# Attention block with f32 products: each product of 128 columns of weights issued as two of 64

## The chip, the cores and the metric

The kernel runs on one core of one Trainium2 chip, in float32 throughout. The metric is the time of one execution in device microseconds. A core has TensorE for matrix products (PE in the profile; its weight loads are listed apart as PEld), VectorE (DVE), ScalarE (ACT), GpSimd (POOL) and the queue of SyncE (SP), which here only issues transfers.

## The reference

An attention block on images: a group norm over 8 groups of channels, the projections to q, k and v, attention with 4 heads over the 1024 pixels of each image, a projection back, and the residual. The input is 16 images of 512 channels by 32 x 32 pixels, so a head has 128 channels.

```python
b, c, h, w = x.shape                      # 16, 512, 32, 32
xg = x.reshape(b, NUM_GROUPS, -1)         # 8 groups
...
xn = ((xg - mu) * jax.lax.rsqrt(var + EPS)).reshape(b, c, h, w)
xn = xn * norm_gamma[:, None, None] + norm_beta[:, None, None]
qkv = jnp.einsum('oc,bchw->bohw', qkv_w, xn) + qkv_b[:, None, None]
q, k, v = jnp.split(qkv, 3, axis=1)
...
scale = dh ** (-0.5)
attn = jax.nn.softmax(jnp.einsum('bhnd,bhmd->bhnm', q, k) * scale, axis=-1)
out = jnp.einsum('bhnm,bhmd->bhnd', attn, v)
out = out.transpose(0, 1, 3, 2).reshape(b, c, h, w)
out = jnp.einsum('oc,bchw->bohw', proj_w, out) + proj_b[:, None, None]
return x + out
```

## The kernel before, in words

The work is a fast path, followed by a general branch that is taken only if a softmax sum left its safe range; the profiled execution does not take it. All that follows is the fast path.

**Attention (L843 to L950).** The main loop runs over 512 steps: 16 images, 4 heads, 8 blocks of 128 keys. A step has two halves of 512 queries. In each half `scores` (L846) multiplies a block of 128 keys, as the weights, with 512 queries, as the moving operand, into a bank of PSUM called `s`; ScalarE takes the exponential of it into `p` (L852); and `weighted_sum` (L942) multiplies a block of `v`, as the weights, with the `p` of the step before, and accumulates over the 8 key blocks in `po`. There are two `s` banks, and one `po` of two banks, which ScalarE copies out to `o` (L949) at the end of a head. VectorE adds up the `p` of a head in `tot` (L858, L860); their sums give the softmax denominators, which are inverted, spread over the partitions by way of DRAM, and multiplied into `o` by VectorE. From the second image on, the blocks of `v` lie with a step of four elements between columns (`v_block`, L793).

**Projections (L472 to L700).** The products with the projection weights for q and k (two sites per image), v and the output are done by a scheme with seven products in place of eight, on two levels. `two_levels` runs four groups of outer products (`OUTER`); in each group `strassen` runs seven units `p1` to `p7` in the order `ORDER`, and `mm` (L606) issues one product per outer product of the group: 128 x 128 weights, 256 moving columns. Units write the PSUM banks called `qk_x`, `qk_y`, `v_x`, `v_y`, `pp_x` and `pp_y`. Between two units ScalarE copies an `x` bank out (`kept_copy`, L486: tiles `qk_p`, `qk_u` and the like) and later units go on accumulating in the same bank. VectorE combines the parts (L630, L679). The v product of the first image is on one level (`v_units`, L732), and so is the output projection of the last one (`last_projection`, L1031, tiles `lx`, `ly`, `lz`).

**Order.** The projections of the next image, and the output projection of the image before, are spread over the main loop by `plan_head`: a list of units for each step of a head, half of which run after each half step. TensorE's instructions are in program order: scores, weighted sum, one or two units, and so on. Copies and exponentials are marked with a raised priority, so that they come early in the order of their engine.

**Small products.** The group norm averages over channels with products of a 128 x 128 matrix `avg` with 2 or 4 columns (L83, L88). `warm` (L1149) issues products of `avg` with itself at the start. `bias_of_v` (L965) and `last_division` (L904, L922) use one or 512 columns of the moving operand. The check for the general branch, on the tile `most` (L1077, L1078), has weights of a single column.

Each call of `nc.tensor.matmul` in f32 gives two weight loads and two passes in the records.

Of the kernel before, what the change touches and what calls it, by code (L numbers as in the profile page):

```python
# [16 lines left out]
P = 128  # L17
# [8 lines left out]


URGENT = 40


class Norm:
# [29 lines left out]
    def group_steps(self, mv, first=0):  # L61


        nc, gn, k = self.nc, self.gn, mv.shape[1]
        t = {}

        def tile_(n):
            t[n] = gn.tile([P, k], F32, tag=n, name=n)
            return t[n]

        def bank(n):
            t[n] = self.ps.tile([P, HALF], F32, tag=self.tag, name=n)[:, :k]
            return t[n]

        def scale():
            ins = nc.vector.tensor_mul(tile_("sc"), t["rstd"], self.gamma[:, first : first + k])
            self.result = t["mu"], t["sc"]
            return ins


        return [
            lambda: nc.vector.tensor_copy(tile_("mean"), mv[:, :, 0]),
            lambda: nc.tensor.matmul(bank("pm"), self.avg, t["mean"], start=True, stop=True),  # L83
            lambda: nc.vector.tensor_sub(tile_("d"), t["mean"], t["pm"]),
            lambda: nc.vector.tensor_mul(tile_("d2"), t["d"], t["d"]),
            lambda: nc.vector.tensor_add(tile_("vv"), t["d2"], mv[:, :, 1]),
            lambda: nc.vector.tensor_copy(tile_("mu"), t["pm"]),
            lambda: nc.tensor.matmul(bank("pv"), self.avg, t["vv"], start=True, stop=True),  # L88
            lambda: nc.vector.tensor_scalar_add(tile_("ve"), t["pv"], EPS),
            lambda: nc.gpsimd.tensor_tensor(  # L90
                tile_("rstd"), t["ve"], self.neghalf[:, :k], ALU.pow
            ),
            scale,
        ]
# [92 lines left out]
def fast_path(ctx, tc, x, sources, out, consts, flag, dims):  # L187
# [335 lines left out]
    def two_levels(name, site, b, blocks, finish, sums="make", homes="BBBB", prepare=None):  # L523
# [58 lines left out]
        def group_units(g):  # L582
            group = OUTER[g]
            n = len(group)
            have = haves[g]

            def weights():
                have["w"] = group_weights(site, g, b == 0 and site in range(PAIRS))

            def load(m):  # L590
                h = homes.find(homes[g], g + 1)
                if sums == "load" and h > 0:
                    nc.sync.dma_start(sum_tile(h, m), inner_kept[b, h, m])

            def inner_sum(m):
                if sums != "load" and m not in have:
                    make_sum(g, m)

            def inner(i, m):
                return inner_block(g, i, m)  # L600

            def mm(acc, j, first):
                an, bn = FACTORS[j]
                t, slot = SLOTS[an]
                for i in range(n):
                    nc.tensor.matmul(  # L606
                        acc[:, ts(i, Q)], have["w"][t][:, i, slot, :], inner(i, bn),
                        start=(first and i == 0), stop=True, skip_group_check=True,
                    )

            def out_(which, a, c=None):
                row, half = int(which[1]) - 1, int(which[2]) - 1
                if g not in R and opening and g == len(OUTER) - 1:

                    t = opool.tile([P, N], F32, tag="o", name=f"{name}_r{g}")
                    R[g] = t.rearrange("p (i r m) -> p i r m", i=1, r=2)
                elif g not in R:
                    R[g] = rpool.tile(
                        [P, 2, 2, HALF], F32, tag=f"r{g % 3}", name=f"{name}_r{g}"
                    )  # L620
                dst = R[g][:, :n, row, ts(half, Q)]

                def view(t):
                    return t[:, : n * Q].rearrange("p (i q) -> p i q", q=Q)

                with tc.high_priority(URGENT):
                    if c is None:
                        nc.scalar.copy(dst, view(a))
                    else:
                        nc.vector.tensor_add(dst, view(a), view(c))  # L630

            p1, p2, p6, p5, p7, p4, p3 = strassen(f"{name}_{g}", mm, out_, n * Q)

            def unit(*steps):
                def one():
                    for f in steps:
                        f()
                    with placed():
                        for _ in range(min(len(pending), 2 if g == len(OUTER) - 1 else 1)):
                            pending.pop(0)()  # L640
                return one

            def end():
                combine(g)
                if g == len(OUTER) - 1:
                    with placed():
                        run(pending)
                    pending.clear()


            return [
                unit(
                    weights, lambda: first_sums((1,)) if g == 0 and sums == "load" else None,
                    lambda: inner_sum("t1"), lambda: inner_sum("t2"), p1,
                ),
                unit(lambda: inner_sum("t3"), p2), unit(lambda: inner_sum("t4"), p6),
                unit(lambda: load("t2"), lambda: ready(g), p5), unit(lambda: load("t1"), p7),
                unit(lambda: load("t3"), p4), unit(lambda: load("t4"), p3, end),
            ]
# [64 lines left out]
    def v_units(b, jj):  # L724
# [3 lines left out]
        def mm(acc, i, first):  # L728
            wi, bn = wv[FACTORS[i][0]], FACTORS[i][1]
            for g in range(2):  # L730
                for k in range(KC):
                    nc.tensor.matmul(  # L732
                        acc[:, ts(g, HC)], xb[b][bn][k][:, ts(2 * jj + g, P)], wi[:, k, :],
                        start=(first and g == 0 and k == 0), stop=(k == KC - 1),
                        skip_group_check=True,
                    )
# [106 lines left out]
    def scores(s, half):  # L843
        b, h, j = where(s)
        sc = ps_s.tile([P, HALF], F32, tag="s", name=f"s_{s}_{half}")
        nc.tensor.matmul(  # L846
            sc, ks[b, h][:, ts(j, P)], qs[b, h][:, ts(half, HALF)], start=True, stop=True
        )
        if half == 0:
            ps[s] = ppool.tile([P, N], F32, tag="p", name=f"p_{s}")  # L850
# [47 lines left out]
    def last_division(b, h):  # L898
# [2 lines left out]
        t = tot.pop((b, h))  # L901
        acc = ps_s.tile([P, HALF], F32, tag="s", name="l_last")
        for j in range(NB):
            nc.tensor.matmul(  # L904
                acc[:, j : j + 1], t[:, ts(j, P)], ones_sq[:, 0:1], start=(j == 0), stop=True,
                skip_group_check=True,
            )
        r = lpool.tile([P, NB], F32, tag="part", name="r_last")
# [10 lines left out]
            )  # L919
        for half in range(NH2):  # L920
            rows = ps_s.tile([P, HALF], F32, tag="s", name=f"rows_{half}")
            nc.tensor.matmul(  # L922
                rows, ones_sq, blocks[:, ts(half, n), :].rearrange("p j q -> p (j q)"),
                start=True, stop=True,
            )
            i = ts(half, HALF)
            nc.vector.tensor_mul(os_[b, h][:, i], os_[b, h][:, i], rows)
# [9 lines left out]
    def weighted_sum(s, half):  # L937
        b, h, j = where(s)
        if j == 0 and half == 0:
            po[b, h] = ps_o.tile([P, N], F32, tag="o", name=f"po_{b}_{h}")  # L940
        i = ts(half, HALF)
        nc.tensor.matmul(  # L942
            po[b, h][:, i], v_block(b, h, j), ps[s][:, i],
            start=(j == 0), stop=(j == NB - 1),
        )
        if j == NB - 1:
            if (b, h) not in os_:
                os_[b, h] = opool.tile([P, N], F32, tag="o", name=f"o_{b}_{h}")
            last_eviction[b] = nc.scalar.copy(os_[b, h][:, i], po[b, h][:, i])  # L949
# [9 lines left out]
    def bias_of_v(o):  # L959
# [2 lines left out]
        half, r = divmod(o, 2)  # L962
        for c in range(NCC):
            block = stage["proj"][f"a{half + 1}{c // KC + 1}"]
            nc.tensor.matmul(  # L965
                acc[:, 0:1], block[:, ts(r * KC + c % KC, P)], vb_sb[:, c : c + 1],
                start=(c == 0), stop=(c == NCC - 1),
            )
        nc.vector.tensor_add(
# [53 lines left out]
    def last_projection(b):  # L1023
# [4 lines left out]

        def mm(acc, r, p, first):
            for k in range(KC):  # L1030
                nc.tensor.matmul(  # L1031
                    acc, late["w"][p][:, ds((r * KC + k) * P, P)], bl[FACTORS[p][1]][k],
                    start=(first and k == 0), stop=(k == KC - 1), skip_group_check=True,
                )

# [38 lines left out]
            add(1, r, 1, kept_["u3", r], False)  # L1074
            add(1, r, 1, y_[r], True)
        most = ps_s.tile([P, HALF], F32, tag="s", name="most")
        nc.tensor.matmul(most[:1, :1], total, ones, start=True, stop=False)  # L1077
        nc.tensor.matmul(most[:1, :1], span, ones_sq[:, 0:1], start=False, stop=True)  # L1078
        ok = gn.tile([1, 1], F32, tag="fine", name="fine")
        nc.vector.tensor_scalar(ok, most[:1, :1], LIMIT, None, ALU.is_le)  # L1080
        fine.append(ok)
# [67 lines left out]
    def warm(n, name):  # L1149

        acc = ps_s.tile([P, HALF], F32, tag="s", name=name)
        for _ in range(n):
            ins = nc.tensor.matmul(acc[:, :P], avg, avg, start=True, stop=True)  # L1153
            tc.keep_in_program_order(ins)

    def open_image():
# [247 lines left out]
```

## Time and profile before

| what | value |
|---|---|
| median of two runs (3171.86 and 3172.45 us) | 3172.15 us |
| span of the profiled execution, first to last instruction | 3170.7 us |
| mean granted TensorE clock in it | 1.000 |
| PE busy, records | 3159.9 us, 10524 |
| PEld busy, records | 2190.7 us, 10524 |
| DVE / ACT / POOL busy | 2633.6 / 1439.7 / 517.7 us |
| mean share of the 16 DMA engines that the two largest queues use | 28.8% and 19.2% |

The profiled execution has a span of its own, 3170.7 us; its whole time is not listed beside it, and the two runs lie 1.2 and 1.8 us above that span. A line of the profile's groups reads: line of the kernel, engine, operation, what is written and read, rows and columns of weights (128\*128), shape of the output, number of records, then the busy time of the group, the mean time of one record, and the idle time of the engine ahead of them with what ended it. Busy times are of the union: records that overlap are counted once, so a mean can be longer than the distance from one start to the next.

### The profile page before, as it was taken

To read this page: it belongs to the slowest core of one execution; us is meant where nothing else is said; L and a number is where in the kernel's file an instruction comes from. 1 tells how busy PE (TensorE), PEld (TensorE's weight loads), DVE (VectorE), ACT (ScalarE), POOL (GpSimd) and SP (SyncE) were. 2 spreads that over 40 slices of the span, in tenths; PEclk is the share of its full clock that TensorE was granted. 3 is DMA by queue.
4 is the path that set the end of the run, shared out by engine and by line. 5 is a ranking of instruction groups with operands and counts; after the bars stand their busy time and mean duration, and the time that the engine had idled before them with its cause. 6 is when DMAs were issued, how large, how long until landed. Compare 5 with 4: busy or idle time off the path is not lost.

```text
span 3170.7 us, 34267 instructions
## 1 busy us (share of the span) xinstructions
PE 3159.9 (100%) x10524; PEld 2190.7 (69%) x10524; DVE 2633.6 (83%) x4639; ACT 1439.7 (45%) x2712; POOL 517.7 (16%) x898
## 2 busy tenths in 40 slices
PE   9999999999999999999999999999999999999999
PEld 7566676677766676777767767677676776766764
DVE  9878879788897888878788787987879978788784
ACT  3535435354353543545435453453534545344342
POOL 0011221111211112211122111222012221122200
PEclk9999999999999999999999999999999999999999
DMA  5554554555545455454554545555455564555531
GB/s 177 185 190 154 188 172 154 171 153 192 171 164 162 153 185 175 167 167 145 191 172 162 171 145 187 171 172 172 144 175 169 176 189 134 174 162 186 179 116 41
DMA packets 210333, 524.32 MB, mean 165 GB/s; under 512 B 32096, under 2 KB 65376, under 8 KB 210144
## 3 DMA queue, kind: packets, MB, share of 16 engines
q1 hardware_dynamic: 132896, 282.12, 28.8%
q0 software_dynamic: 64000, 204.54, 19.2%
q10 hardware_dynamic: 13248, 35.39, 3.5%
q8 instruction: 87, 1.43, 0.2%
q14 instruction: 102, 0.84, 0.1%
HBM read 388.77 MB, written 133.17 MB: 165 GB/s over the span
## 4 chain that ended last, share of the span: by engine, by line
PE 96%; DVE 3%; DMA 0%; issue 0%; POOL 0%; SPq 0%; ACT 0%; DVEq 0%; POOLq 0%
PE po L942 27%; PE s L846 27%; PE qk_x L606 12%; PE qk_y L606 9%; PE pp_x L606 6%; PE v_x L606 6%; PE pp_y L606 4%; PE v_y L606 4%; PE lx L1031 0%; DVE qk_t L574 0%; PE ly L1031 0%; PE warm L1153 0%; DVE tot L860 0%; DVE qk L714 0%; DVE qk_r L630 0%
## 5 line engine op out<-in xcount | busy, mean ns | idle before, releaser
L942 PE MATMUL po<-p,v 128*128 128x512 f32 x2048 | 1049.5, 594 | 0.7 <-ACT p L852 0.7
L846 PE MATMUL s<-qk,qk 128*128 128x512 f32 x2048 | 1047.4, 593 | 0.3 <-DVE qk L714 0.3
L852 ACT ACTIVATE p<-s 128x512 f32<-128x512 f32 x1024 | 610.9, 597 | 961.0 <-PE s L846 957.2
L942 PEld LDWEIGHTS po<-p,v 128*128 128x128 f32 x2048 | 603.6, 302 | 322.7 <-issue 214.5
L860 DVE TENSOR_TENSOR tot<-tot,p 128x1024 f32<-128x1024 f32 x385 | 469.0, 1218 | 158.4 <-ACT p L852 156.3
L846 PEld LDWEIGHTS s<-qk,qk 128*128 128x128 f32 x2048 | 387.7, 190 | 88.6 <-issue 29.9
L606 PEld LDWEIGHTS qk_x<-qk_t,w 128*128 128x128 f32 x1344 | 251.8, 190 | 166.1 <-issue 75.3
L606 PE MATMUL qk_x<-qk_t,w 128*128 128x256 f32 x1344 | 356.3, 382 | 0.1
L486 ACT COPY qk_u<-qk_x 128x512 f32<-128x512 f32 (+1 forms) x256 | 136.3, 533 | 229.2 <-PE qk_x L606 229.2
L779 POOL DMA_DIRECT2D vd<-vu x120 | 66.7, 557 | 899.8 <-DVE vu L771 897.9
L630 DVE TENSOR_TENSOR qk_r<-qk_y,qk_u 128x512 f32<-128x512 f32 (+1 forms) x256 | 157.7, 616 | 34.7 <-ACT qk_u L486 21.6
L580 POOL DMA_DIRECT2D kept_t<-qk_t x240 | 129.4, 540 | 278.4 <-DVE qk_t L574 211.9
L606 PEld LDWEIGHTS pp_x<-pp_t,w_proj 128*128 128x128 f32 x630 | 117.2, 190 | 74.7 <-issue 32.3
L784 POOL DMA_DIRECT2D v<-vd x240 | 140.6, 593 | 167.1 <-DMA vd<-vu 70.3
L630 DVE TENSOR_TENSOR v_r<-v_y,v_u 128x512 f32<-128x512 f32 (+1 forms) x120 | 76.0, 633 | 110.6 <-ACT v_u L486 80.3
L606 PE MATMUL pp_x<-pp_t,w_proj 128*128 128x256 f32 x630 | 167.8, 383 | 0.0
L606 PE MATMUL v_x<-v_t,w_v 128*128 128x256 f32 x630 | 166.6, 381 | 0.0
L830 POOL DMA_DIRECT2D out_y<-y x120 | 66.0, 550 | 604.2 <-DVE y L829 602.4
L606 PEld LDWEIGHTS v_x<-v_t,w_v 128*128 128x128 f32 x630 | 118.4, 190 | 55.3 <-issue 19.1
L606 PE MATMUL qk_y<-x,w 128*128 128x256 f32 x512 | 142.1, 379 | 0.0
L714 DVE SCALAR_TENSOR_TENSOR qk<-qk_r,qkb_sb,qk_r 128x512 f32<-128x512 f32 x192 | 137.5, 743 | 1.6
L486 ACT COPY v_u<-v_x 128x512 f32<-128x512 f32 (+1 forms) x124 | 66.3, 535 | 157.1 <-PE v_x L606 130.3
(217 smaller groups left out, 4487.2 us busy)
## 6 DMA issues: line engine op xcount, KB each, us to landing
w<-kept SPq DMA_DIRECT2D x90, 512.0 KB, 3.7
kept_t<-qk_t POOLq DMA_DIRECT2D x180, 256.0 KB, 3.3
v_t<-kept_t SPq DMA_DIRECT2D x180, 256.0 KB, 2.9
w<-kept SPq DMA_DIRECT2D x90, 384.0 KB, 3.4
rinv<-row ACTq DMA_DIRECT2D x63, 512.0 KB, 4.9
x<-in_x POOLq DMA_DIRECT2D x60, 512.0 KB, 4.6
vd<-vu POOLq DMA_DIRECT2D x120, 256.0 KB, 3.1
v<-vd POOLq DMA_DIRECT2D x240, 128.0 KB, 4.2
```

What stands on the lines that cost most here:

```text
L486: nc.scalar.copy(t[n][:, :width], t["x"][:, :width])
L580: nc.gpsimd.dma_start(t, to)
L606: nc.tensor.matmul(acc[:, ts(i, Q)], have["w"][t][:, i, slot, :], inner(i, bn), start=(first and i == 0), stop=True, skip_group_check=True,)
L630: nc.vector.tensor_add(dst, view(a), view(c))
L714: nc.vector.scalar_tensor_tensor(st[b, h][:, ts(half, HALF)], a, qkb_sb[:, i : i + 1], c, ALU.add, ALU.add)
L779: nc.gpsimd.dma_start(rows[which][ts(h, P), :], u)
L784: nc.gpsimd.dma_start(vs[b, pair][ts(q, BLK), half].rearrange("m h (k i) j -> m (h k) (i j)", k=n), rows[which].rearrange("(k m) (q e) -> ...
L830: nc.gpsimd.dma_start(out[b, ts(o, P), ts(half, HALF)], t)
L846: nc.tensor.matmul(sc, ks[b, h][:, ts(j, P)], qs[b, h][:, ts(half, HALF)], start=True, stop=True)
L852: exps[s] = nc.scalar.activation(ps[s][:, ts(half, HALF)], sc, AF.Exp, scale=SCALE)
L860: added[b, h, j] = nc.vector.tensor_add(tot[b, h][:, i], tot[b, h][:, i], ps[s][:, i])
L942: nc.tensor.matmul(po[b, h][:, i], v_block(b, h, j), ps[s][:, i], start=(j == 0), stop=(j == NB - 1),)
```

## The change

A helper takes the place of `nc.tensor.matmul` in the fast path. Where the weights have 128 columns it issues two products: columns 0 to 63 of the weights into partitions 0 to 63 of the output, then columns 64 to 127 into partitions 64 to 127, with the same moving operand and the same flags. Weights with fewer than 128 columns (the two products on `most`) are issued as before. The instruction that it returns is the second of the two. The general branch keeps its calls.

```diff
+def halves_of(nc, out, lhsT, rhs, **flags):
+
+    m = lhsT.shape[-1]
+    if m < P:
+        return nc.tensor.matmul(out, lhsT, rhs, **flags)
+    for d in range(2):
+        cols = ts(d, P // 2)
+        ins = nc.tensor.matmul(out[cols], lhsT[:, cols], rhs, **flags)
+    return ins
...
-            lambda: nc.tensor.matmul(bank("pm"), self.avg, t["mean"], start=True, stop=True),
+            lambda: halves_of(nc, bank("pm"), self.avg, t["mean"], start=True, stop=True),
...
                 for i in range(n):
-                    nc.tensor.matmul(
-                        acc[:, ts(i, Q)], have["w"][t][:, i, slot, :], inner(i, bn),
+                    halves_of(
+            nc, acc[:, ts(i, Q)], have["w"][t][:, i, slot, :], inner(i, bn),
                         start=(first and i == 0), stop=True, skip_group_check=True,
                     )
...
-        nc.tensor.matmul(
-            sc, ks[b, h][:, ts(j, P)], qs[b, h][:, ts(half, HALF)], start=True, stop=True
+        halves_of(
+            nc, sc, ks[b, h][:, ts(j, P)], qs[b, h][:, ts(half, HALF)], start=True, stop=True
         )
...
-        nc.tensor.matmul(
-            po[b, h][:, i], v_block(b, h, j), ps[s][:, i],
+        halves_of(
+            nc, po[b, h][:, i], v_block(b, h, j), ps[s][:, i],
             start=(j == 0), stop=(j == NB - 1),
         )
...
-            ins = nc.tensor.matmul(acc[:, :P], avg, avg, start=True, stop=True)
+            ins = halves_of(nc, acc[:, :P], avg, avg, start=True, stop=True)
```

The same replacement is made in the second averaging product (L88), in `v_units`, `last_division`, `bias_of_v` and `last_projection`.

More of the change, by code (lines that the diff above doesn't have):

```diff
@@ L87, in group_steps @@
             lambda: nc.vector.tensor_copy(tile_("mu"), t["pm"]),
-            lambda: nc.tensor.matmul(bank("pv"), self.avg, t["vv"], start=True, stop=True),
+            lambda: halves_of(nc, bank("pv"), self.avg, t["vv"], start=True, stop=True),
             lambda: nc.vector.tensor_scalar_add(tile_("ve"), t["pv"], EPS),
@@ L731, in mm @@
                 for k in range(KC):
-                    nc.tensor.matmul(
-                        acc[:, ts(g, HC)], xb[b][bn][k][:, ts(2 * jj + g, P)], wi[:, k, :],
+                    halves_of(
+            nc, acc[:, ts(g, HC)], xb[b][bn][k][:, ts(2 * jj + g, P)], wi[:, k, :],
                         start=(first and g == 0 and k == 0), stop=(k == KC - 1),
@@ L903, in last_division @@
         for j in range(NB):
-            nc.tensor.matmul(
-                acc[:, j : j + 1], t[:, ts(j, P)], ones_sq[:, 0:1], start=(j == 0), stop=True,
+            halves_of(
+            nc, acc[:, j : j + 1], t[:, ts(j, P)], ones_sq[:, 0:1], start=(j == 0), stop=True,
                 skip_group_check=True,
@@ L921, in last_division @@
             rows = ps_s.tile([P, HALF], F32, tag="s", name=f"rows_{half}")
-            nc.tensor.matmul(
-                rows, ones_sq, blocks[:, ts(half, n), :].rearrange("p j q -> p (j q)"),
+            halves_of(
+            nc, rows, ones_sq, blocks[:, ts(half, n), :].rearrange("p j q -> p (j q)"),
                 start=True, stop=True,
@@ L941, in weighted_sum @@
         i = ts(half, HALF)
-        nc.tensor.matmul(
-            po[b, h][:, i], v_block(b, h, j), ps[s][:, i],
+        halves_of(
+            nc, po[b, h][:, i], v_block(b, h, j), ps[s][:, i],
             start=(j == 0), stop=(j == NB - 1),
@@ L964, in bias_of_v @@
             block = stage["proj"][f"a{half + 1}{c // KC + 1}"]
-            nc.tensor.matmul(
-                acc[:, 0:1], block[:, ts(r * KC + c % KC, P)], vb_sb[:, c : c + 1],
+            halves_of(
+            nc, acc[:, 0:1], block[:, ts(r * KC + c % KC, P)], vb_sb[:, c : c + 1],
                 start=(c == 0), stop=(c == NCC - 1),
@@ L1030, in mm @@
             for k in range(KC):
-                nc.tensor.matmul(
-                    acc, late["w"][p][:, ds((r * KC + k) * P, P)], bl[FACTORS[p][1]][k],
+                halves_of(
+            nc, acc, late["w"][p][:, ds((r * KC + k) * P, P)], bl[FACTORS[p][1]][k],
                     start=(first and k == 0), stop=(k == KC - 1), skip_group_check=True,
@@ L1076, in last_projection @@
         most = ps_s.tile([P, HALF], F32, tag="s", name="most")
-        nc.tensor.matmul(most[:1, :1], total, ones, start=True, stop=False)
-        nc.tensor.matmul(most[:1, :1], span, ones_sq[:, 0:1], start=False, stop=True)
+        halves_of(nc, most[:1, :1], total, ones, start=True, stop=False)
+        halves_of(nc, most[:1, :1], span, ones_sq[:, 0:1], start=False, stop=True)
         ok = gn.tile([1, 1], F32, tag="fine", name="fine")
```

## Prediction

> **What bounds the kernel now.** I read the page's busy shares and its row of the granted clock first, then the chain that ended last, then the costliest groups, and at the end three stretches of the timeline for the price of one pass.
>
> ```profile
> span 3170.7 us, 34267 instructions
> PE 3159.9 (100%) x10524; PEld 2190.7 (69%) x10524; DVE 2633.6 (83%) x4639; ACT 1439.7 (45%) x2712; POOL 517.7 (16%) x898
> ...
> PE 96%; DVE 3%; DMA 0%; issue 0%; POOL 0%; SPq 0%; ACT 0%; DVEq 0%; POOLq 0%
> ...
> L942 PE MATMUL po<-p,v 128*128 128x512 f32 x2048 | 1049.5, 594 | 0.7 <-ACT p L852 0.7
> L846 PE MATMUL s<-qk,qk 128*128 128x512 f32 x2048 | 1047.4, 593 | 0.3 <-DVE qk L714 0.3
> L852 ACT ACTIVATE p<-s 128x512 f32<-128x512 f32 x1024 | 610.9, 597 | 961.0 <-PE s L846 957.2
> L942 PEld LDWEIGHTS po<-p,v 128*128 128x128 f32 x2048 | 603.6, 302 | 322.7 <-issue 214.5
> ```
>
> TensorE is the bound in every slice: busy for 3159.9 of 3170.7 us, 96% of the chain, its two largest groups idle for 1.0 us together, the mean granted clock 1.000. ScalarE waits for TensorE (957.2 us), not the other way round. So anything that lengthens a product lengthens the kernel almost one for one, and nothing on another engine can give time back. There are 1024 calls in each attention line and 2048 records: an f32 product is two passes, each with a weight load of its own. The 594 ns are a pass from start to end, with the next one already begun; what a pass costs is the distance between starts:
>
> ```profile
> 19.03 3.62 PE L732 MATMUL v_z<-wv_a,x 128*128 128x256 f32 x16
> 22.49 3.62 PE L732 MATMUL v_x<-wv_s,xt 128*128 128x256 f32 x16
> ```
>
> Sixteen passes of 256 columns from 19.03 to 22.49 us are 216 ns each. In the chain, sixteen passes of 512:
>
> ```profile
> 3150.87 6.87 PE lx L1031 x16
> ```
>
> That is 429 ns each. 256 columns more cost 213 ns, so 512 are 426 ns of streaming and a pass has about 3 ns of its own. **The stock of passes** from the groups: 4156 of 512 columns (2048 at L846, 2048 at L942, 56 at L1031, 4 at L922), 6188 of 256 (6076 at L606, 112 at L732), 180 short ones. 4156 x 0.429 + 6188 x 0.216 + 180 x 0.112 = 1783 + 1337 + 20 = 3140 us; the missing 20 us of busy time are passes that started late.
>
> **The change, part by part.** `halves_of` replaces each product of 128 columns of weights by two of 64, on output partitions 0 to 63 and 64 to 127. It takes nothing away: both halves stream all 256 or 512 columns of the moving operand. It adds one product, so two passes and two loads, to each of 5172 long products (4156/2 + 6188/2). Call the passes A1, A2 (first half) and B1, B2 (second half). Where they run decides everything, and no row of this trace shows two column tiles at work.
>
> *The streaming.* Bounds: if passes on different column tiles never run together, the stream time doubles, 1783 + 1337 = +3120 us, and with late starts more; if they run together wholly, +0. Passes start in order, so A2 waits for A1 (same tile), B1 starts with A2, B2 waits for B1, and the next product's A1 starts with B2: each pass time then carries two passes, and a product still takes two pass times. I take +0: the halves touch separate weights and separate output partitions, and nothing in the order A1 A2 B1 B2 keeps neighbours on different tiles apart.
>
> The Trainium skill, "TensorE: Matmul & The Clock Gate", Part 3, has three column tiles of 32 columns at 2.38 times the speed of one after another, with some 4 ns between starts; no run here shows that, and it says nothing of f32 passes.
>
> *The change of tile.* Each product now has two starts that follow a start on the other tile (B1 after A2, A1 after B2). Each such start comes a little after its partner and pushes all that follows. Lower bound: the 3 ns that a pass has of its own. Upper bound: the closest two starts anywhere in the trace, in the tiny products on `most`:
>
> ```profile
> 3157.67 0.19 PE L1077 MATMUL most<-ones,total 32*1 32x1 f32 x2
> ```
>
> Two passes of 160 ns (their own row) take 0.19 us together, so their starts are some 26 ns apart. Those two share one tile, and the streamed pass has its weights already loaded as here, so I take 3 ns: 5172 x 2 x 3 = **+31 us** (0 at least, 269 us at 26 ns).
>
> By the skill's 4 ns on the same page this term would be 41 us.
>
> *The weight loads.* Twice as many, half as wide. The products of one column show what a load of 128 columns costs when nothing else limits it:
>
> ```profile
> 3140.34 1.75 PEld L904 LDWEIGHTS l_last<-ones_sq,tot 128*128 128x128 f32 x15 [0.24 <-issue]
> ```
>
> Less the last one's 0.19 us, 14 starts in 1.56 us: 111 ns apart. Half the columns I estimate at 56 ns, between that and 111 if a load has no part that shrinks. Two loads per pass time are 112 ns, at most 222, under a 512-column pass (429) and a 256-column pass (216): hidden at the value taken, at the upper end 6 ns over for 256 columns (6188 x 6 = 37 us). The loads of `v` at L942 (302 ns, strided, some 220 without the 80 ns that a load of one column takes at L1078) stay within 429 as well. So +0, bounds 0 and 37. What is lost without that cover is the second rival.
>
> *Issue.* TensorE's queue carries twice the instructions: eight in the 432 ns of a 256-column product, 54 ns each. In the row above two instructions pass every 111 ns, 56 ns each, but these are held by the load; the pair on `most` passes in 26 ns. I take +0; at 56 ns it would be 3094 products x 16 ns = 50 us, and below 0 there is nothing to gain.
>
> *Later ends.* With the order above, a product's second half ends one pass time later than before, 216 or 429 ns, with the same start. Exps have room (ScalarE idles 961 us ahead of them); the inner products copy one bank and write into it again soon, and there TensorE's loads already wait:
>
> ```profile
> PEld qk_x L606 <- ACT qk_u L486: 36.0, 71, 0.6
> PEld pp_x L606 <- ACT pp_u L486: 16.2, 30, 0.6
> PEld v_x L606 <- ACT v_u L486: 16.2, 30, 0.6
> PEld v_y L606 <- DVE v_r L630: 13.5, 30, 0.8
> ```
>
> 161 waits with no room left. A pass time later each is 161 x 0.216 = 35 us at most, 0 if the wait sits on another, earlier product. I take half, **+17 us**. What is queued behind is the whole of TensorE's queue, and behind it exp, so it counts in full.
>
> *Ends and rest.* The last product ends 0.43 us later and so do its add and transfer: +0.4. The warming products and other short ones are held by loads of 111 ns, two halves of 56 cost the same: 0. No transfer, no step of VectorE, ScalarE or GpSimd changes; they have 17%, 55% and 84% of the span free.
>
> **Sum.** 3170.7 + 31 + 17 + 0.4 = 3219 us of span; the runs' median lies 1.45 us above the profiled span, so **3221 us**, 1.5% more. Nearly everything the change adds is hidden under the other tile's pass.
>
> **Rivals.** *First, one after another (slower).* If the second half's passes start only when the first half's have streamed, whether because f32 passes don't share the array or because both halves are put in the same place (the change then doesn't do what it says), the place is every long product and the price one pass time per added pass: +3120 us of streaming, and 20 us of late starts kept as they are. 3172 + 3120 = **6292 us**, to 6345 with late starts that double and a few starts in excess. For it: the trace has nothing but one pass after another, 429 and 216 ns apart without exception in long runs. Against: nothing shows that the array as a whole is what a pass holds, since every long pass here fills all 128 columns.
>
> *Second, weights one load ahead only (slower).* In the timeline a load begins when the pass before its own begins, never earlier:
>
> ```profile
> 1505.37 0.59 PE L606 MATMUL pp_x<-o,w_proj 128*128 128x256 f32 x2
> 1505.37 0.19 PEld L606 LDWEIGHTS pp_x<-o,w_proj 128*128 128x128 f32 x1 [0.24 <-issue]
> ```
>
> If B1's load can't start until A2 has, B1 follows A2 by a load (56 ns, for strided `v` about 110) instead of 3, and so does A1 after B2: 960 products with strided `v` x 2 x 0.11 + 4212 x 2 x 0.056 = 211 + 472 = +683 us, **3855 us**. It decides as soon as such a load isn't ahead of the pass that is waiting. The 26 ns of `most` at every change of tile instead give 3172 + 269 = **3441 us**. For both: one load ahead is all the trace shows. Against: with one tile a second load had nowhere to go; with two there is a free place.
>
> The Trainium skill, the same page, Part 2, lets loads be pulled ahead where row groups don't conflict or the background buffer is the target; both halves here use all rows, so only the second holds. The row at 1505.37 agrees with it for one tile.
>
> *A gain* would need a pass that streams faster in a tile of 64 columns; the clock is at 1.000 and a pass is streaming but for 3 ns, so I leave it 2 in 100.
>
> **How the numbers follow.** Together, as summed: 46 in 100, of which 30 stay within 2% of 3172 us (below 3235.6) and 16 pass it, by more late starts or issue (own range 3172 to 3300 us). Start costs of 26 ns to a load: 19 (3300 to 4000). One after another: 33. Gain over 2%: 2. 2% is about what a measurement of this kernel can surely tell from no change. So faster 0.02, same 0.30, slower 0.68; the likeliest single case is the sum. Without the doubled case a range would leave out a third, so it runs from 3172 to 6345 us.
>
> **What would show it.** Right: 64-column records on PE, about 21,000, starts in pairs 3 ns apart, 429 or 216 ns from pair to pair, the span within 50 us of before. Second rival: starts alternating between a pass time and a pass time plus some 56 ns, loads ending just ahead of them. First rival: starts 429 or 216 ns apart one by one, all other engines at half their shares. The forecast is wrong if the PE starts of one `s` product lie further apart than 2 x 429 plus some 20 ns.

## The result, and the profile after

The changed kernel takes 3301.21 us (two runs, 3299.91 and 3302.51) against 3172.15 us, a ratio of 1.0406 with a 95% interval of 1.0376 to 1.0436: 129 us slower. The predicted 3221 us had the right sign, but its 49 us are less than half of the loss.

The page of the changed kernel; all products now have line L38, that of the helper, and other lines have moved by 11:

```profile
span 3300.7 us, 55325 instructions
PE 3242.4 (98%) x21044; PEld 2004.1 (61%) x21044; DVE 2663.9 (81%) x4639; ACT 1451.8 (44%) x2712; POOL 505.5 (15%) x898
...
PE 87%; DVE 10%; issue 1%; ACT 1%; DMA 1%; SPq 0%; POOL 0%; ACTq 0%; DVEq 0%; POOLq 0%
...
L38 PE MATMUL s<-qk,qk 128*64 128x512 f32 x4096 | 1597.7, 593 | 0.4 <-DVE qk L725 0.4
L38 PE MATMUL po<-p,v 128*64 128x512 f32 x4096 | 1593.6, 593 | 0.7 <-ACT p L863 0.7
L863 ACT ACTIVATE p<-s 128x512 f32<-128x512 f32 x1024 | 611.5, 597 | 950.5 <-PE s L38 943.3
L38 PEld LDWEIGHTS po<-p,v 128*64 128x64 f32 x4096 | 675.9, 190 | 369.6 <-issue 300.2
```

There are twice the passes, each as long as before (593 ns from start to end), in a span 4% longer, so the tiles do stream side by side. But TensorE no longer makes up nearly all of the chain: 87% where it was 96%, with 10% on VectorE. Its own waits, by who ended them, were 1.5 us or less in every row before (the row's three numbers are us in total, times, and the longest):

```profile
PE warm L1153 <- DVE avg L248: 1.5, 1, 1.5
```

Now:

```profile
PE qk_x L38 <- ACT qk_u L497: 23.5, 47, 0.6
PE v_x L38 <- ACT v_u L497: 9.3, 15, 0.6
PE v_y L38 <- DVE v_r L641: 4.6, 15, 0.4
PE pp_x L38 <- ACT pp_u L497: 4.4, 15, 0.4
```

These rows count only time in which both tiles stood still. For each tile by itself I worked from the starts of the records: taken in order, each pass goes to the tile whose last pass is over (429 ns after its start for 512 columns, 216 ns for 256), and what lies between is a gap. No pass ever finds both tiles busy, and the gaps add up to some 152 us on one tile and 157 us on the other; the kernel before has some 28 us on its one. The difference, 124 and 129 us, is all or nearly all of the loss of 129 us. (The sums move by a few us with the time that one allows for the short products, the differences hardly.) Of it, some 200 gaps longer than 0.2 us hold 125 and 130 us; the kernel before has 11 such gaps, worth 4 us.

Here is a place in the kernel before without such a gap (start and length in us; a bracket is idle time and what ended it):

```profile
177.41 1.03 PE L606 MATMUL qk_x<-qk_t,w 128*128 128x256 f32 x4
178.27 1.02 PE L846 MATMUL s<-qk,qk 128*128 128x512 f32 x2
178.47 0.59 ACT L486 COPY qk_u<-qk_x 128x512 f32<-128x512 f32 x1 [1.12 <-PE qk_x L606]
179.13 1.11 PE L606 MATMUL qk_x<-qk_t,w 128*128 128x256 f32 x4
```

The same place in the changed kernel has one of the long gaps:

```profile
183.60 0.75 PE L38 MATMUL qk_x<-qk_t,w 128*64 128x256 f32 x3
...
184.03 0.59 PE L38 MATMUL s<-qk,qk 128*64 128x512 f32 x1
184.19 0.59 PE L38 MATMUL qk_x<-qk_t,w 128*64 128x256 f32 x2
...
184.46 0.59 PE L38 MATMUL s<-qk,qk 128*64 128x512 f32 x1
...
184.62 0.38 PE L38 MATMUL qk_x<-qk_t,w 128*64 128x256 f32 x1
...
185.03 0.59 ACT L497 COPY qk_u<-qk_x 128x512 f32<-128x512 f32 x1 [1.12 <-PE qk_x L38]
...
185.67 1.08 PE L38 MATMUL qk_x<-qk_t,w 128*64 128x256 f32 x8 [0.62 <-ACT qk_u L497]
...
186.59 0.59 PE L38 MATMUL s<-qk,qk 128*64 128x512 f32 x1
```

A unit on `qk_x` ends, ScalarE copies that bank out (L486 before, L497 now), and the next unit writes into the bank again, at 179.13 before and at 185.67 now. In the kernel before a whole product on `s`, 0.86 us, stands between the two units and covers the copy of 0.59 us. In the changed kernel its first half alone (two passes on one tile, 184.03 and 184.46) stands there; its second half comes after the next unit, at 186.59. So both tiles wait for the copy, each some 0.8 us.

The built program shows why. A planner orders the instructions of each engine before the run. In the order of the changed kernel the halves of 227 of the 5260 halved products stand apart, with other products between them, and 775 of 2723 places on ScalarE and 2441 of 4576 on VectorE hold another instruction than before. In some 125 of the 227 it is a product on `s` that has a unit of the inner products between its halves, as in the place shown. A program that issues the first halves alone is put into exactly the order of the kernel before on all five engines. So to the planner a half is as long as a whole, and with both halves it must take TensorE to be twice as slow.

### The profile page after: what moved, and what is told of

It reads as the page before. It is cut to its first block, busy times and chain, and to the rows that moved or that the text cites. A ratio compares the mean times of both kernels' runs of the same rounds, so it can differ in the third digit from the quotient of the medians.

```text
span 3300.7 us, 55325 instructions
## 1 busy us (share of the span) xinstructions
PE 3242.4 (98%) x21044; PEld 2004.1 (61%) x21044; DVE 2663.9 (81%) x4639; ACT 1451.8 (44%) x2712; POOL 505.5 (15%) x898
## 4 chain that ended last, share of the span: by engine, by line
PE 87%; DVE 10%; issue 1%; ACT 1%; DMA 1%; SPq 0%; POOL 0%; ACTq 0%; DVEq 0%; POOLq 0%
PE s L38 27%; PE po L38 22%; PE qk_x L38 12%; PE qk_y L38 8%; PE pp_x L38 5%; PE v_x L38 4%; PE pp_y L38 4%; PE v_y L38 4%; DVE tot L871 1%; DVE vu L782 1%; DVE o L963 1%; ACT qk_u L497 1%; DVE v_r L641 1%; DVE pp_r L641 1%; DVE vt L779 1%
## 5 line engine op out<-in xcount | busy, mean ns | idle before, releaser
L38 PE MATMUL s<-qk,qk 128*64 128x512 f32 x4096 | 1597.7, 593 | 0.4 <-DVE qk L725 0.4
L38 PE MATMUL po<-p,v 128*64 128x512 f32 x4096 | 1593.6, 593 | 0.7 <-ACT p L863 0.7
L38 PEld LDWEIGHTS po<-p,v 128*64 128x64 f32 x4096 | 675.9, 190 | 369.6 <-issue 300.2
L38 PEld LDWEIGHTS s<-qk,qk 128*64 128x64 f32 x4096 | 462.4, 137 | 132.8 <-issue 42.1
L38 PE MATMUL qk_x<-qk_t,w 128*64 128x256 f32 x2688 | 505.0, 382 | 24.2 <-ACT qk_u L497 23.5
L38 PEld LDWEIGHTS qk_x<-qk_t,w 128*64 128x64 f32 x2688 | 297.5, 137 | 185.0 <-issue 63.5
L38 PE MATMUL v_x<-v_t,w_v 128*64 128x256 f32 x1260 | 266.3, 381 | 9.3 <-ACT v_u L497 9.3
L497 ACT COPY qk_u<-qk_x 128x512 f32<-128x512 f32 (+1 forms) x256 | 136.6, 534 | 240.9 <-PE qk_x L38 237.7
L38 PE MATMUL qk_y<-x,w 128*64 128x256 f32 x1024 | 225.3, 380 | 1.1 <-DVE qk_r L641 1.1
L38 PE MATMUL pp_x<-pp_t,w_proj 128*64 128x256 f32 x1260 | 199.7, 386 | 5.4 <-ACT pp_u L497 4.4
L38 PEld LDWEIGHTS v_x<-v_t,w_v 128*64 128x64 f32 x1260 | 138.9, 136 | 73.0 <-ACT v_u L497 24.5
L38 PE MATMUL qk_y<-qk_t,w 128*64 128x256 f32 x896 | 180.9, 379 | 0.0
L38 PE MATMUL qk_y<-xt,w 128*64 128x256 f32 x768 | 160.9, 379 | 0.0
L38 PEld LDWEIGHTS pp_x<-pp_t,w_proj 128*64 128x64 f32 x1260 | 95.7, 136 | 101.8 <-issue 34.3
```

What stands on the lines that cost most here:

```text
L38: ins = nc.tensor.matmul(out[cols], lhsT[:, cols], rhs, **flags)
L497: nc.scalar.copy(t[n][:, :width], t["x"][:, :width])
```

## The experiments

**One: the halves, in the order of before.** Every product is still two halves. At the end of the fast path, each instruction of an engine is pinned behind the one that precedes it in the order of the kernel before (an order of issue, with no wait), the two halves of a product next to each other. With whole products the same pins give the program of the kernel before, instruction for instruction.

```diff
     nc.vector.tensor_scalar(flag, fine[0], -1.0, 1.0, ALU.mult, ALU.add)
+    stand(tc)
...
+        chain = [i for p in places for i in lists[engine][p]]
+        for a, b in zip(chain, chain[1:]):
+            tc.add_manual_dep(
+                b, a.name,
+                mybir.DependencyInfo(
+                    mybir.DependencyClass.NoSync, mybir.DependencyReason.DATA
+                ),
```

> All products still in two halves, but the instructions of all five engines stand in exactly the order that they have in the kernel before, the second half right behind the first. Theory A (the planner's new order costs the time: it put other products between the halves of 227 products and moved copies and sums on ScalarE and VectorE): the two tiles run side by side for nothing, so 3175 to 3195 us, ratio 1.001 to 1.007. Theory B (a product's second half ends up to a pass time later, whatever the order, and the consumers pass this on): the roughly 200 long waits of some 0.65 us stay, 3270 to 3310 us, ratio 1.03 to 1.045.

Measured: 3164.08 us, ratio 0.9974 (0.9965 to 0.9984). The loss is gone, and 8 us more, which is below the 3175 to 3195 us that I gave theory A. Its page:

```profile
span 3163.4 us, 55387 instructions
PE 3150.3 (100%) x21044; PEld 1601.7 (51%) x21044; DVE 2635.9 (83%) x4639; ACT 1440.3 (46%) x2712; POOL 518.4 (16%) x898
```

The same place of the same head in its timeline:

```profile
179.08 1.06 PE L72 MATMUL qk_x<-qk_t,w 128*64 128x256 f32 x8
179.94 1.06 PE L72 MATMUL s<-qk,qk 128*64 128x512 f32 x4
180.81 1.08 PE L72 MATMUL qk_x<-qk_t,w 128*64 128x256 f32 x8
```

The unit, the whole `s` product in four passes, and the next unit start 0.86 and 0.87 us apart, with no wait between them. Theory B is out: the later end of a second half costs nothing that shows. Gaps per tile are some 23 us, about a dozen of them over 0.2 us. This version beats both kernels, the one before by a quarter of a percent.

**Two: the changed kernel's order, with the halves put together.** The same pins with the order of the changed kernel on all engines, except that each second half follows its first.

```diff
         ins = nc.tensor.matmul(out[cols], lhsT[:, cols], rhs, **flags)
+        made.append(ins.ins)
+    PRODUCTS.append(made)
     return ins
```

Products are pinned by these lists, so a list stands together, at the place of its first half.

> The changed kernel with its own order on VectorE, ScalarE, GpSimd and SyncE and its own order of first halves on TensorE; only the 227 second halves that stood apart are put right behind their first half. If the parted halves are what costs (theory A1): the wait for the copy of a bank is covered by the whole attention product again, 3180 to 3210 us. If the moved copies and sums on ScalarE and VectorE cost (theory A2), or the later ends (theory B): 3270 to 3310 us.

Measured: 3210.96 us, ratio 1.012 (1.0103 to 1.0137). Putting 227 halves back takes away 90 of the 129 us. The value is 1 us above theory A1's range, and what stays, 47 us over experiment one, is for something else: the other engines' order, or the 232 of 5262 places on TensorE where the first halves too stand in another order than before.

**Three: whole products, the new order on the other engines.** TensorE in its order of before with 128 columns; VectorE, ScalarE, GpSimd and SyncE in the changed kernel's order.

```diff
-        ins = nc.tensor.matmul(out[cols], lhsT[:, cols], rhs, **flags)
+        ins = nc.tensor.matmul(out, lhsT, rhs, **flags)
```

> Products of 128 columns as before and TensorE's order of before, but VectorE, ScalarE, GpSimd and SyncE in the order of the changed kernel. It prices that order without any halves. Theory A1 (parted halves) and theory B (later ends): 3172 to 3185 us. Theory A2 (the order elsewhere): a good part of the 129 us, 3220 us or more.

Measured: 3218.48 us, ratio 1.0144 (1.0127 to 1.0161): 46 us without a single half and with TensorE's order of before, just short of the 3220 us that I gave theory A2. Its largest waits of TensorE:

```profile
PE v_y L68 <- DVE v_r L673: 11.7, 15, 0.8
PE pp_x L68 <- ACT pp_u L529: 9.3, 14, 0.7
PE po L68 <- ACT o L992: 7.1, 14, 0.5
```

The rows on `v_y` and on `po` are the two largest that experiment two has left as well (16.3 and 8.9 us); the one on `pp_x` is not in its list. So theory A holds with both its parts: 3164 + 47 (order of the other engines) + 90 (parted halves) = 3301 us. That sum closes by itself, as its terms are the differences of these runs; what confirms it is that the 46 us of experiment three, found with whole products, agree with the 47. So the 232 places on TensorE add next to nothing.

**Four: all first halves of a unit, then all second halves,** with the order of before otherwise.

```diff
-                for i in range(n):
-                    halves_of(
-            nc, acc[:, ts(i, Q)], have["w"][t][:, i, slot, :], inner(i, bn),
...
+    for d in range(2):
+        cols = ts(d, P // 2)
+        for (out, lhsT, rhs, flags), mine in zip(products, made):
+            ins = nc.tensor.matmul(out[cols], lhsT[:, cols], rhs, **flags)
```

> As the run with the order of before, but in each unit of the inner products that has two products (1302 units) first both first halves are issued, then both second halves: four passes on one tile, then four on the other. If passes start strictly in the order of the program, as the prediction had it, a unit takes six pass times in place of four: 1302 x 2 x 0.2155 = +561 us over the run with the order of before. If each tile takes its passes from the queue on its own, past passes that wait for the other tile: the same time as that run, within 15 us.

Measured: 3169.09 us, ratio 0.9992 (0.9982 to 1.0001), 5 us over experiment one where a strict order would have cost 561 us. In the records, set beside the order of the built program, the first pass on the second tile starts together with the first one on the other, some 1300 times, ahead of three passes that stand before it in the program and wait for that other tile. The changed kernel's timeline shows the same in small:

```profile
15.29 0.38 PE L38 MATMUL v_y<-wv_s,x 128*64 128x256 f32 x1
15.49 0.38 PE L38 MATMUL v_x<-wv_a,x 128*64 128x256 f32 x1
```

The first pass on `v_y` starts 0.2 us ahead of the last one on `v_x`, which stands before it in the program. The Trainium skill, "TensorE: Matmul & The Clock Gate", Part 3, has products start and end strictly in order; between column tiles these starts and the 5 us speak against it.

**Five: four quarters of 32 columns,** in the order of before.

```diff
-    for d in range(2 if m == P else 1):
-        cols = ts(d, P // 2) if m == P else slice(0, m)
+    for d in range(4 if m == P else 1):
+        cols = ts(d, P // 4) if m == P else slice(0, m)
```

> The order of before on all engines, each product of 128 columns now as four of 32 columns on four column tiles. The run with halves in that order came out 8 us under the kernel before, with the same stream time per tile; its late starts behind a load that was not ahead are near 46 ns in place of 84. Theory S (that gain is the shorter load that is seen when a bank's copy comes late): a load of 32 columns shows some 28 ns, about 150 late starts by 18 ns less and the like, 3157 to 3164 us. Theory O (that gain has another source, such as chance in where the waits fall): 3160 to 3175 us. Theory I (issue binds: sixteen instructions in the 432 ns of a 256-column product, 27 ns each, where the closest two starts in the trace were 26 ns apart): if an instruction takes 30 ns or more, 3094 x 48 ns = +149 us or more, over 3310 us.

Measured: 3166.3 us, ratio 0.9985 (0.9976 to 0.9994). Issue does not bind even with four times the products:

```profile
PE 3148.6 (100%) x42084; PEld 1399.5 (44%) x42084; DVE 2638.9 (83%) x4639; ACT 1440.4 (46%) x2712; POOL 516.8 (16%) x898
```

But it brings nothing over halves, and theory S had it at 3164 us or less. The gaps per tile are again 23 us. So the shorter load as the source of the 8 us is not confirmed. It isn't refuted either: among the passes of 256 and 512 columns the late starts under 0.2 us fall from 11.5 to 8.9 us on a tile, and the longer waits grow from 7 to 10 us. What the starts show is that from the kernel before to experiment one the gaps fall from 28 to 23 us, where some 170 late starts of 84 ns (14.5 us) have become some 150 of 46 ns (7 us); what the other 3 of the 8 us are stays open.

**Six: halves for the inner products alone,** in the order of before. Products with 512 moving columns keep 128 columns of weights.

```diff
     m = lhsT.shape[-1]
+    two = m == P and rhs.shape[-1] == Q
     made = []
-    for d in range(2 if m == P else 1):
+    for d in range(2 if two else 1):
```

> The order of before on all engines; only the products with 256 moving columns are halved, those with 512 keep 128 columns of weights. TensorE then changes between tiles of 64 and of 128 columns 2157 times. If a change of tile shape lets the array run empty and hides no load (112 ns from the last start to the first load of the other shape beside the products on most, and 56 to 112 ns of load): 2157 x 0.1 to 0.3 us = +216 to +650 us, 3380 to 3820 us. If a product of 128 columns only waits until both tiles are free: half a pass offset at most for each change, 0 to 2157 x 0.1 us, 3164 to 3380 us, the more likely the lower end.

Measured: 3556.22 us, ratio 1.1211 (1.1193 to 1.1228), 392 us over experiment one and inside the range for an array that runs empty and hides no load. Its timeline around one visit to the tiles of 64 columns:

```profile
1500.73 1.08 PE L73 MATMUL qk_x<-qk_t,w 128*64 128x256 f32 x8
1501.75 1.12 PE L73 MATMUL s<-qk,qk 128*128 128x512 f32 x2
1502.71 0.59 PE L73 MATMUL po<-p,v 128*128 128x512 f32 x1
```

Eight passes that fill 0.86 us take 1.02 us to the next start, and two passes of 512 columns take 0.96 in place of 0.86 us. In the starts, a pass after a change from 128 to 64 columns comes 522 ns after its predecessor in place of 429, and no load is ahead of it. Over some 1092 visits, a stay on the small tiles is 0.153 us and one on the large tile 0.197 us longer than its passes (medians): 1092 x 0.35 = 382 of the 392 us. This is what an array that runs empty at each change of tile shape would give; the records show the 93 ns and the load in the open, not the array itself. The Trainium skill, "TensorEngine Tiling (Array Packing)", Key Properties, says that changing the tiling mode drains the engine; the 93 ns and the exposed load agree with it.

**Seven: TensorE in the order of the kernel's text.** The changed kernel, each product pinned behind the one traced before it; the other engines are left to the planner.

```diff
-        ins = nc.tensor.matmul(out[cols], lhsT[:, cols], rhs, **flags)
+        ins = PINS[-1](nc.tensor.matmul(out[cols], lhsT[:, cols], rhs, **flags))
```

> The changed kernel with every product pinned behind the one traced before it, so that the halves stay together and TensorE keeps the order in which the kernel's text issues its products; the other four engines are left to the planner, which counts a half as long as a whole. The order of the other engines cost 46 us with whole products and 47 us with adjacent halves, the parted halves 90 us. If that holds for this order too: 3205 to 3225 us, ratio 1.010 to 1.017, which is 75 to 95 us under the changed kernel. If the traced order of TensorE itself leaves waits that the planner used to fill: 3230 us or more. If the planner, tied to one order on TensorE, places the other engines as well as before: 3164 to 3175 us.

Measured: 3329.32 us, ratio 1.0498 (1.048 to 1.0515), slower than the changed kernel. The halves are together, and the waits for the copies are back all the same, the largest on the output projection:

```profile
PE pp_x L41 <- ACT pp_u L501: 43.2, 30, 2.5
PE qk_x L41 <- ACT qk_u L501: 37.0, 64, 0.7
```

My expected 3205 to 3225 us took the price of the parted halves as a thing of its own. It depends on what stands between a unit and the next on the same bank, and these waits say that the traced order is worse in that. The run doesn't part it from the rest, though: the other engines' order is again another than before (981 of 2723 places on ScalarE, 2649 of 4576 on VectorE, more than in the changed kernel).

## Why the prediction was wrong

**Streaming, +0: right.** The tiles work side by side. With the order held, 21044 passes take what 10524 took, so the rival "one after another" is out.

**The change of tile, +31 us: wrong, it is 0.** The sum rested on passes starting in the program's order, each start on the other tile pushing all that follow. Experiment four shows that the tiles don't hold to that order between them, so an offset between two tiles is there once and does not add up: in experiment one nearly all halves start 5 to 8 ns after their partner, more than the 3 ns of the sum, and it costs nothing. For the same reason the second rival (3855 or 3441 us) fails: in the changed kernel a tile's passes come 429 or 216 ns apart wherever it hasn't just waited for data.

**Weight loads, +0, and issue, +0: right,** by experiments one and five.

**Later ends, +17 us, 35 at most: wrong.** With the order of before the gaps are not longer than with whole products. The rows of loads that waited for copies, from which I had taken 161 tight places, do point to the banks where the changed kernel loses time; but the cause is another.

**The step that failed is one that the sum does not have.** I held the order of instructions on every engine fixed ("with the same start"; "no step of VectorE, ScalarE or GpSimd changes"). The order is a planner's, worked out from its own durations, and the change doubles those of TensorE while the chip's stay. (The description's "TensorE's instructions are in program order" misleads here too: in the kernel before, 682 of 5262 products stand at another place than in the kernel's text.) Parted halves cost 90 us and the other engines' new order 47 us, 137 together; with the 8 us that the halves gain, that is the measured 129. The case I had named for 16 in 100, more than 2% by "more late starts or issue", had the right look and no mechanism, and its own range ended at 3300 us. The whole range, up to 6345 us, held the measured time only because it was stretched for the case of one after another. The second rival's range began at 3300 us, so the time falls on its edge by chance: the alternating starts that it asked for are not there.

## What to carry to other kernels

Where a planner orders the instructions, a change that alters its idea of a duration alters the order on every engine; hold the old order and measure again before giving the chip the blame. On an engine that is full, price what stands between two uses of the same buffer: the 227 parted halves cost 90 us here, 0.4 us each on average and twice that in the place shown. Splitting a product over column tiles that are full together neither costs nor gains stream time, and mixing tile shapes costs 0.35 us for each visit.

## What the runs showed of the hardware

- Two column tiles with f32 passes stream side by side without loss over a whole kernel, and four do too (3164 and 3166 us, with 21044 and 42084 passes).
- The two tiles are not held to the program's order between them: a pass starts ahead of three older ones that wait for the other tile (5 us where strict order would have cost 561).
- A change between tiles of 64 and of 128 columns delays the next pass by 93 ns and leaves its load in the open: 0.35 us for there and back.
